# VectorE's order in the q and k blocks, eighteen convolutions of v around their end, and ranks by one comparison per pair

## The chip, the core and the metric

The kernel runs on one core of a Trainium2 chip. The metric is the device time of one execution in microseconds. The engines are TensorE (PE in the profile, its weight loads PEld), VectorE (DVE), ScalarE (ACT), GpSimd (POOL) and SyncE (SP), each with an instruction queue of its own; transfers are issued from the queues of SP, ACT and POOL and run on 16 DMA engines.

## The reference, cut to what matters

The input x is one image of 384 channels and 192 × 192 pixels, float32. Two layers follow one another, each a residual branch on a group norm (32 groups).

```python
# layer 0
qkv = einsum('bchw,oc->bohw', gn(x), w_qkv) + b_qkv          # 1x1 convolution, 384 -> 1152
qkv = qkv.reshape(b, 3*c, 96, 2, 96, 2).max(axis=(3, 5))     # 2x2 max pooling
qkv = depthwise3x3(qkv, w_dw) + b_dw
q, k, v = split(qkv)                                         # 8 heads of 48 channels
q, k = q / max(norm(q), 1e-12), k / max(norm(k), 1e-12)      # norms over the 9216 pixels
attn = einsum('bhcn,bhdn->bhcd', q, k) * temperature         # 48 x 48 per head
out = sum(a_i * topk_softmax(attn, kk) @ v for kk in (24, 32, 36, 38))
x = x + proj(upsample2x(gelu(out)))
# layer 1
x = x + depthwise7x7(gn(x), mean of the four rotations of the weight)
```

`topk_softmax` keeps the kk largest entries of a row; of equal entries the earlier one comes first.

## The kernel before, in words

Channels lie on partitions, 384 of them as three tiles (KT = 3). After the statistics of the first norm (to about 167 us) the norm's scale is folded into `wq`, and q and k are computed in 24 blocks of eight image rows. A block has six channel tiles (three of q, three of k). For each, `pooled` runs three groups of 512 pixels (L663, three matmuls each into a PSUM tile `pq`, of which there are four buffers) and a reduce on VectorE (L673) that takes the maximum of four pixels and writes it into that channel tile's `ring`, a buffer of three blocks of pooled rows with borders. `bordered` has ScalarE copy a row from one end of the ring to the other where it wraps (L695, when the block's number is divisible by three; L699). One block later the nine taps of the depthwise convolution run on VectorE (L706 the first, L708 the eight others). Then comes a 32 × 32 transpose on VectorE (L791), the sum of squares on ScalarE (L719), and, once three tiles of q or of k are there, sixteen copies on ScalarE (`turned`, L725) that complete the transposition into `qkT`. `products` multiplies q by k for pairs of heads into the accumulator `grams` (L741, 24 records per block); they are woven one by one between the matmuls of L663 two blocks later.

`keep` fixes an instruction's place in its engine's order. `pinned` calls it for PE alone: PE's order is written by hand, VectorE's, ScalarE's and GpSimd's orders come from a scheduler that works with modelled times. `issue_after` keeps an instruction from being placed ahead of another.

After the 24th block, the round with b = NB finishes the last taps and starts v. `convolve` is one convolution of v: six matmuls for two strips of two image rows and one channel tile into a `pv` tile (L549, 12 records, two buffers) and one pooling reduce on VectorE into `rows` (L555, called an eviction below). A row group of v is nine such convolutions. The first six stand in the round b = NB, among the last taps; 21 more, up to three row groups (AHEAD = 3), are called together with the steps of `attention`, a generator:

- the norms of q and k and the temperature (L825 to L836), with two small groups of matmuls on PE (L832, L232);
- `scaled` (L841) out of `grams`, ten DMAs that gather the heads' 48 × 48 blocks into `att`, issued in turn from GpSimd and ScalarE, and the scores (L847);
- the rank of each of the 48 entries in its row: for each of three channel tiles five VectorE operations on 48 × 48 = 2304 elements per partition (L866 to L874);
- maximum, exponential (ScalarE), four masked and normalised softmaxes added into `mix` (L879 to L897);
- ten DMAs that lay `mix` out as the block diagonal matrix `diag`, and its transposition on PE into `aT` (L910), evicted as `attnT`.

Between these the scheduler also places the first taps of v (`depthwise_v`, L959 and L963). With `attnT`, a loop over the 16 row groups follows (v, attention, gelu, projection, residual L1076), and then layer 1, in which PE runs the 7 × 7 convolution as matmuls with band matrices (L1482).

Of the kernel before, what the change touches and what calls it, by code (L numbers as in the profile page):

```python
# [8 lines left out]
F32 = mybir.dt.float32  # L9
# [77 lines left out]
def conv_preact_d2(  # L87
# [138 lines left out]
    def along_free(dst, src, pool, name, tag=None):  # L226

        ps = pool.tile([P, C], F32, name=f"af_{name}", tag=tag or f"af_{name}")
        for t in range(KT):
            dg = const.tile([P, P], F32, name=f"dg_{name}_{t}", tag="dg", bufs=KT)  # L230
            nc.vector.tensor_scalar_mul(dg, ident, src[:, t : t + 1])
            nc.tensor.matmul(ps[:, t * P : (t + 1) * P], ones, dg, start=True, stop=True)  # L232
        nc.vector.tensor_copy(dst, ps)
# [329 lines left out]
    with ExitStack() as bx:  # L563
# [78 lines left out]
        def pinned(ins):  # L642

            if ins.ins.engine != mybir.EngineType.PE:
                return ins
            keep(ins)
            while between and next(between[0], between) is between:
# [3 lines left out]
        def pooled(b, ct, xb):  # L651
# [3 lines left out]
            for g in range(3):  # L655
# [17 lines left out]
                nc.vector.tensor_reduce(  # L673
# [4 lines left out]
                )  # L678

# [21 lines left out]
        def taps(dst, ct, win):  # L701
            for tap in range(9):
                src = win(tap // 3, tap % 3)
                w = wd[:, ct, tap : tap + 1]
                if tap == 0:
                    nc.vector.tensor_scalar(dst, src, w, bdb[:, ct : ct + 1], ALU.mult, ALU.add)  # L706
                else:
                    nc.vector.scalar_tensor_tensor(dst, src, w, dst, ALU.mult, ALU.add)  # L708

        def depthwise(b, ct, dst):  # L710
            r0 = b % 3 * PR
            taps(dst, ct, lambda i, j: ring[ct][:, r0 + i : r0 + i + PR, j : j + PS])
# [45 lines left out]
        multiplied = None  # L758
        for b in range(NB + 1):
            xb = None  # L760
            if b < NB:
                xb = held.pop(b) if b in held else load_x(b, "xq")
            else:
# [3 lines left out]
                xb = xpool.tile([P, 2 * UT, KT, RB * HW], F32, name="xv_begun", tag="xb")  # L767
                for kt in range(KT):
                    nc.sync.dma_start(xb[:, :, kt], image_rows(kt, order[0], 0, 2 * UT))
            done, sides = sides, []  # L770
            for ct in range(2 * KT + 1):
                if ct == (KT if b < NB else 1) and done:
                    between.append(products(b - 2, done))
                if b < NB and ct < 2 * KT:
                    if b == 0 and ct < 2:

                        if ct == 0:
                            pooled(b, 0, xb)
                            pooled(b, 1, xb)
                            biases()  # L780
                    else:
                        pooled(b, ct, xb)
                    bordered(b, ct)
                if b > 0 and ct > 0:
                    dst = qkp.tile([P, PR, PS], F32, name=f"qk{b}_{ct}", tag="qk")
                    depthwise(b - 1, ct - 1, dst)
                    s, t = divmod(ct - 1, KT)
                    if t == 0:
                        turns = trp.tile([P, KT, PB], F32, name=f"turns{b}_{s}", tag=f"turns{s}")
                    flat = dst.rearrange("p h w -> p (h w)")  # L790
                    nc.vector.transpose(turns[:, t], flat)  # L791
                    squares(b - 1, ct - 1, flat)

                    for _ in copies:
                        pass
                    if t == KT - 1:
                        side = trp.tile([P, PB // P, C], F32, name=f"qkT{b}_{s}", tag=f"qkT{s}")
                        sides.append(side)
                        copies = turned(side, turns)
                        for _ in range(2):  # L800
                            next(copies)
                    if b == NB:
                        for n in ((), (), (0, 1), (), (2, 3), (4,), (5,))[ct]:
                            t0 = n // KT * UT
# [773 lines left out]
```

## Time and profile before

| what | value |
|---|---|
| median of 3 runs | 2787.28 us (2781.11 to 2789.88) |
| the profiled execution | 2786.69 us, span 2784.9 us |
| mean TensorE clock granted | 0.985 |
| busy PE / DVE / ACT / POOL | 2591.1 / 2456.2 / 1140.1 / 746.7 us |
| q and k: last matmul of L663 ends | 1316.4 us |
| scores (L847) | 1373.16 us |
| attention matrix on PE (L910) starts | 1451.85 us |

A line of a timeline gives the start and the length in us, engine, line and operation, the tile written and the tiles read, shapes, the number of instructions merged into the line, and in brackets how long the engine was idle just before and whose end released it. A group line of the page gives busy us, mean ns of one instruction, and the idle time just before. All times in the text count from the start of the span. A record of L549 or L663 is half a matmul on float32, so that 12 records make a convolution.

### The profile page before, as it was taken

The numbers are of one execution on the slowest core, as the hardware profiler recorded it, in microseconds if no ns is written. First come the engines' busy times: TensorE is split into PE (matmuls) and PEld (weight loads), VectorE is DVE, ScalarE is ACT, GpSimd is POOL, SyncE is SP. The second block draws the span as 40 slices with busy tenths as digits, with TensorE's granted clock in tenths as the row PEclk, the third lists the DMA queues.
The fourth block names the chain that finished last, engine by engine and source line by source line (L and its number), as shares of the span: only waits on it lengthen the run. The fifth ranks groups of instructions, "written<-read, shape, count | busy, mean of one in ns | idle before, by whom it ended". The sixth has DMA issues, their size and how long they took to land. (4 is left out here: it accounts for less than half of the span.)

```text
span 2784.9 us, 25837 instructions
## 1 busy us (share of the span) xinstructions
PE 2591.1 (93%) x8365; PEld 1525.2 (55%) x8365; DVE 2456.2 (88%) x3527; ACT 1140.1 (41%) x2262; POOL 746.7 (27%) x885
## 2 busy tenths in 40 slices
PE   0399999999999999999899969999999899999998
PEld 0144444444444444444556646666666677777776
DVE  7989998989999999999789958999889789888886
ACT  0143423333343333433402312232323577777776
POOL 1024443100000000000111321010101478787876
PEclk9999999999999999999899989999999999999999
DMA  9976766301010110110336997566674899999998
GB/s 381 402 252 217 249 213 228 130 34 68 35 68 35 40 62 35 68 35 0 120 103 238 340 362 231 192 230 219 203 246 151 324 343 366 372 375 372 372 374 264
DMA packets 234039, 581.01 MB, mean 209 GB/s; under 512 B 16640, under 2 KB 165744, under 8 KB 217136
## 3 DMA queue, kind: packets, MB, share of 16 engines
q1 hardware_dynamic: 173408, 283.44, 29.0%
q0 software_dynamic: 37376, 148.85, 15.8%
q10 hardware_dynamic: 23120, 147.07, 14.1%
q8 instruction: 67, 1.10, 0.2%
q14 instruction: 68, 0.56, 0.1%
HBM read 370.93 MB, written 208.21 MB: 208 GB/s over the span
## 5 line engine op out<-in xcount | busy, mean ns | idle before, releaser
L663 PE MATMUL pq<-xq,wq 128*128 128x512 f32 x2268 | 1028.8, 597 | 5.4 <-DVE ring L673 4.7
L708 DVE SCALAR_TENSOR_TENSOR qk<-ring,wd,qk 128x384 f32<-128x384 f32 x1152 | 699.4, 616 | 59.5 <-ACT ring L695 32.1
L663 PEld LDWEIGHTS pq<-xq,wq 128*128 128x128 f32 x2268 | 408.7, 190 | 437.3 <-issue 364.0
L549 PE MATMUL pv<-xv,wq 128*128 128x384 f32 x1656 | 545.7, 490 | 26.0 <-DMA xv<-in_x_dram 21.7
L549 PEld LDWEIGHTS pv<-xv,wq 128*128 128x128 f32 x1656 | 316.7, 192 | 245.8 <-issue 20.4
L1482 PE MATMUL pc<-main,w 128*128 128x288 f32 x1536 | 436.4, 406 | 3.0 <-PE al L1515 1.7
L1502 DVE TENSOR_SCALAR apart<-pc,rb 32x576 f32<-32x576 f32 x384 | 312.1, 813 | 81.2 <-PE pc L1482 55.4
L1482 PEld LDWEIGHTS pc<-main,w 128*128 128x128 f32 x1536 | 290.6, 190 | 87.1 <-issue 2.4
L725 ACT COPY qkT<-turns 32x288 f32<-32x288 f32 x768 | 329.0, 428 | 20.7 <-DVE turns L791 9.3
L1500 ACT ACTIVATE apart<-pc,rb 32x576 f32<-32x576 f32 x384 | 281.1, 732 | 133.5 <-PE pc L1482 128.7
L959 DVE SCALAR_TENSOR_TENSOR vb<-rows,wd,vb 128x576 f32<-128x576 f32 x384 | 313.3, 817 | 11.3
L673 DVE TENSOR_REDUCE ring<-pq 128x128 f32<-128x512 f32 x428 | 292.1, 683 | 3.7 <-PE pq L663 3.6
L1482 PE MATMUL pc<-aux,h 128*128 128x288 f32 x768 | 248.1, 405 | 0.0
L719 ACT ACTIVATE junk<-qk 128x384 f32<-128x384 f32 x144 | 71.1, 494 | 411.8 <-DVE qk L708 411.0
L1441 POOL COPY res<-apart 128x1152 f32<-128x1152 f32 (+1 forms) x96 | 222.0, 2338 | 13.3 <-ACT apart L1500 9.5
L826 POOL TENSOR_TENSOR rn<-rn,halfpos 128x6 f32<-128x6 f32 x1 | 1.4, 1359 | 827.5 <-DVE rn L825 827.5
L1076 DVE TENSOR_TENSOR sx<-xr,y 128x576 f32<-128x576 f32 x180 | 203.8, 1173 | 19.9 <-ACT y L1047 14.8
L555 DVE TENSOR_REDUCE rows<-pv 128x192 f32<-128x768 f32 x144 | 137.7, 957 | 84.7 <-PE pv L549 84.6
L1117 POOL DMA_DIRECT2D sd<-sx x96 | 72.2, 755 | 514.5 <-DVE sx L1076 493.2
L741 PEld LDWEIGHTS grams<-qkT,qkT 128*96 128x96 f32 x576 | 92.8, 165 | 147.3 <-issue 136.1
L1096 ACT ACTIVATE wq<-sx,negmid 128x1152 f32<-128x1152 f32 x96 | 120.6, 1257 | 122.5 <-DVE sx L1076 118.2
L1482 PEld LDWEIGHTS pc<-aux,h 128*128 128x128 f32 x768 | 145.1, 189 | 41.2 <-issue 0.2
(227 smaller groups left out, 2270.6 us busy)
## 6 DMA issues: line engine op xcount, KB each, us to landing
sd<-sx POOLq DMA_DIRECT2D x96, 600.0 KB, 10.1
out_dram<-res SPq DMA_DIRECT2D x192, 288.0 KB, 11.2
main<-sd ACTq DMA_DIRECT2D x46, 1200.0 KB, 6.7
xv<-in_x_dram SPq DMA_DIRECT2D x138, 384.0 KB, 6.6
xr<-in_x_dram SPq DMA_DIRECT2D x45, 1152.0 KB, 11.7
xq<-in_x_dram SPq DMA_DIRECT2D x21, 2304.0 KB, 8.2
w<-wt ACTq DMA_DIRECT2D x46, 1024.0 KB
xs<-in_x_dram SPq DMA_DIRECT2D x24, 1536.0 KB, 15.1
```

The source lines that it names most:

```text
L549: nc.tensor.matmul(ps[:, u, 0 : RB * HW], wq[:, kt, o : o + P], xb[:, u, kt, :], start=(kt == 0), stop=(kt == KT - 1),)
L555: nc.vector.tensor_reduce(rows[ct][:, 1 + t0 : 1 + t0 + UT, 1 : PS + 1], ps[:, :, 0 : RB * HW].rearrange("p u (a w b) -> p u w a b", a=2, ...
L663: ins = nc.tensor.matmul(ps, wq[:, kt, ct * P : (ct + 1) * P], rows[:, kt, :, g * 64 : (g + 1) * 64], start=(kt == 0), stop=(kt == KT - 1) ...
L673: nc.vector.tensor_reduce(t[:, r0 : r0 + PR, 1 + g * 32 : 1 + (g + 1) * 32], ps.rearrange("p (h a w b) -> p h w a b", h=PR, a=2, b=2), AX. ...
L708: nc.vector.scalar_tensor_tensor(dst, src, w, dst, ALU.mult, ALU.add)
L725: nc.scalar.copy(side[f * Q : (f + 1) * Q].rearrange("p c (t n) -> p t c n", n=P)[:, :, :, a * Q : (a + 1) * Q], turns[a * Q : (a + 1) * Q ...
L959: pin(nc.vector.scalar_tensor_tensor(dst, src, w, dst, ALU.mult, ALU.add))
L1076: nc.vector.tensor_tensor(bass.AP(flat.tensor, flat.offset + at(e) + a * RUN, [flat.ap[0], [JP, NT], [1, NJ], [at(f) - at(e), 2]],), xq[:, ...
L1441: keep(copy(res[ps, k], apart[ps, :, k].rearrange("p e n -> p n e")))
L1482: nc.tensor.matmul(ahead[q][:, k, 0 : NT * NJ], lhs, rhs, start=(j == 0), stop=(j == 2), skip_group_check=True,)
L1500: keep(nc.scalar.mul(dst, src, scale))
L1502: keep(nc.vector.tensor_scalar_mul(dst, src, scale))
```

## The change

- **q and k, from the third block on.** `pinned` keeps VectorE's instructions too. The taps are now a generator (`depthwise`), and `pooled` takes two taps after each of its three reduces. The remaining three taps and the transpose of a channel tile (`finish`) come after the next tile's three reduces and six taps. The products join PE's order at the fifth channel tile of a block in place of the fourth. `qkT` of q gets a second buffer.
- **The end of q and k.** Three tiles of `xpool` are filled with x for two whole row groups of v (18 DMAs on SP in place of 3). In the round b = NB each channel tile's nine taps are split four and five, with a convolution after each part (12), `finish` follows one tile late, two convolutions follow the last `finish`, then the norms (moved here out of `attention`), the last products, and four convolutions whose evictions are not kept in place. The products of the block before last join at the third channel tile. Only the third row group's nine convolutions remain beside `attention`.
- **Ranks.** A row of 48 is split in two halves of 24. One comparison of every entry of the second half with every one of the first (576 elements) is summed along both axes; inside the halves one comparison (1152 elements), masked by `lower`, is summed along both axes. Ranks come from these sums and the constant `after`, the number of later entries.

```diff
         def pinned(ins):
-            if ins.ins.engine != mybir.EngineType.PE:
-                return ins
             keep(ins)
-            while between and next(between[0], between) is between:
+            while ins.ins.engine == mybir.EngineType.PE and between and next(between[0], between) is between:
                 between.pop(0)
             return ins
-        def pooled(b, ct, xb):
+        def pooled(b, ct, xb, taps):
             rows = xb.rearrange("p t (r c) -> p t r c", c=HW)
             t = ring[ct]
             r0 = 1 + b % 3 * PR
...
                     )
                     if b > 1:
                         pinned(ins)
-                nc.vector.tensor_reduce(
+                ins = nc.vector.tensor_reduce(
                     t[:, r0 : r0 + PR, 1 + g * 32 : 1 + (g + 1) * 32],
                     ps.rearrange("p (h a w b) -> p h w a b", h=PR, a=2, b=2),
                     AX.XY,
                     ALU.max,
                 )
+                if b > 1:
+                    pinned(ins)
+                some(taps, 2)
...
-        def taps(dst, ct, win):
+        def depthwise(b, ct, dst, pin):
+            r0 = b % 3 * PR
             for tap in range(9):
-                src = win(tap // 3, tap % 3)
+                i, j = divmod(tap, 3)
+                src = ring[ct][:, r0 + i : r0 + i + PR, j : j + PS]
                 w = wd[:, ct, tap : tap + 1]
                 if tap == 0:
-                    nc.vector.tensor_scalar(dst, src, w, bdb[:, ct : ct + 1], ALU.mult, ALU.add)
+                    pin(
+                        nc.vector.tensor_scalar(
+                            dst, src, w, bdb[:, ct : ct + 1], ALU.mult, ALU.add
+                        )
+                    )
                 else:
-                    nc.vector.scalar_tensor_tensor(dst, src, w, dst, ALU.mult, ALU.add)
-        def depthwise(b, ct, dst):
-            r0 = b % 3 * PR
-            taps(dst, ct, lambda i, j: ring[ct][:, r0 + i : r0 + i + PR, j : j + PS])
+                    pin(nc.vector.scalar_tensor_tensor(dst, src, w, dst, ALU.mult, ALU.add))
+                yield
+        def some(taps, n):
+            for _ in range(n):
+                next(taps, None)
...
+        def finish(b, ct, dst, taps, now=False):
+            nonlocal copies, turns
+            some(taps, 9)
+            s, t = divmod(ct, KT)
+            if t == 0:
+                turns = trp.tile([P, KT, PB], F32, name=f"turns{b}_{s}", tag=f"turns{s}")
+            flat = dst.rearrange("p h w -> p (h w)")
+            ins = nc.vector.transpose(turns[:, t], flat)
+            if b > 0:
+                pinned(ins)
+            for _ in copies:
+                pass
+            squares(b, ct, flat)
+            if t == KT - 1:
+                side = trp.tile(
+                    [P, PB // P, C], F32, name=f"qkT{b}_{s}", tag=f"qkT{s}", bufs=2 - s
+                )
+                sides.append(side)
+                copies = turned(side, turns)
+                for _ in range(4 if now else 2):
+                    next(copies)
+        rn = const.tile([P, 2 * KT], F32, name="rn")
+        rkb = const.tile([P, C], F32, name="rkb")
+        def norms():
...
                 pv = psx.enter_context(tc.tile_pool(name="pv", bufs=2, space=PSUM))
...
+                for n in range(3):
+                    t = xpool.tile([P, 2, UT, KT, RB * HW], F32, name=f"xv_begun{n}", tag="xb")
+                    for k in range(2):
+                        i, t0 = divmod((2 * n + k) * UT, NT)
+                        for kt in range(KT):
+                            nc.sync.dma_start(t[:, k, :, kt], image_rows(kt, order[i], t0, UT))
+                        xvb += [(i, t0, ct, t[:, k]) for ct in range(KT)]
+            for ct in range(2 * KT):
+                dst, taps = None, iter(())
+                if b > 0:
+                    dst = qkp.tile([P, PR, PS], F32, name=f"qk{b}_{ct}", tag="qk")
+                    taps = depthwise(b - 1, ct, dst, pinned if b > 1 else lambda ins: ins)
+                if b < NB:
+                    if ct == KT + 1 and b > 1:
+                        done, sides = sides[0:2], sides[2:]
+                        between.append(products(b - 2, done))
                     if b == 0 and ct < 2:
                         if ct == 0:
-                            pooled(b, 0, xb)
-                            pooled(b, 1, xb)
+                            pooled(b, 0, xb, taps)
+                            pooled(b, 1, xb, taps)
                             biases()
                     else:
-                        pooled(b, ct, xb)
+                        pooled(b, ct, xb, taps)
                     bordered(b, ct)
...
+                if last is not None:
+                    finish(*last)
+                    last = None
+                if b > 0:
+                    last = b - 1, ct, dst, taps
+                if b == NB:
+                    if ct == KT - 1:
+                        between.append(products(b - 2, sides[0:2]))
+                    some(taps, 4)
+                    convolve(*xvb.pop(0), pinned)
+                    some(taps, 5)
+                    convolve(*xvb.pop(0), pinned)
+            if b == NB:
+                finish(*last, True)
+                for _ in range(2):
+                    convolve(*xvb.pop(0), pinned)
+                norms()
+                for _ in products(b - 1, sides[2:4]):
+                    pass
+                for args in xvb:
+                    convolve(*args, pe_keep)
...
+        with tc.issue_after(scores.ins):
+            nc.vector.tensor_reduce(after, lower.rearrange("p d e -> p e d"), AX.X, ALU.add)
+        firsts = ap.tile([P, KT, HH], F32, name="firsts")
+        seconds = ap.tile([P, KT, HH], F32, name="seconds")
+        before, behind = [ap.tile([P, KT, HC], F32, name=n) for n in ("before", "behind")]
+        for mt in range(KT):
+            full = [P, HH, HH]
+            sq = ap.tile(full, F32, name=f"sq{mt}", tag="sq")
+            nc.vector.tensor_tensor(
+                sq,
+                att[:, mt, 0:HH].unsqueeze(1).to_broadcast(full),
+                att[:, mt, HH:].unsqueeze(2).to_broadcast(full),
+                ALU.is_ge,
+            )
+            yield
+            nc.vector.tensor_reduce(seconds[:, mt], sq, AX.X, ALU.add)
+            nc.vector.tensor_reduce(
+                firsts[:, mt], sq.rearrange("p d e -> p e d"), AX.X, ALU.add
+            )
+            yield
+            full = [P, 2, HH, HH]
+            halves = att[:, mt, :].rearrange("p (s d) -> p s d", s=2)
+            tri = ap.tile(full, F32, name=f"tri{mt}", tag="tri")
+            nc.vector.tensor_tensor(
+                tri, halves.unsqueeze(2).to_broadcast(full),
+                halves.unsqueeze(3).to_broadcast(full), ALU.is_ge,
+            )
+            yield
+            nc.vector.tensor_tensor(
+                tri, tri, lower.unsqueeze(1).to_broadcast(full), ALU.mult
+            )
+            yield
+            for t, order in ((before, "p s d e -> p s d e"), (behind, "p s d e -> p s e d")):
+                nc.vector.tensor_reduce(
+                    t[:, mt].rearrange("p (s d) -> p s d", s=2), tri.rearrange(order), AX.X,
+                    ALU.add,
+                )
+                yield
+        nc.vector.tensor_tensor(rank, before, behind, ALU.subtract)
+        halves = rank.rearrange("p t (s d) -> p (t s) d", s=2)
+        nc.vector.tensor_tensor(
+            halves, halves, after.unsqueeze(1).to_broadcast([P, 2 * KT, HH]), ALU.add
         )
...
+        nc.vector.tensor_tensor(rank[:, :, HH:], rank[:, :, HH:], seconds, ALU.add)
+        nc.vector.scalar_tensor_tensor(
+            rank[:, :, 0:HH], rank[:, :, 0:HH], float(HH), firsts, ALU.add, ALU.subtract
+        )
+        yield
...
+        for _ in range(9):
+            next(chain, None)
+        i = AHEAD - 1
+        for t0 in range(0, NT, UT):
+            xb = load_v(i, t0)
+            with tc.issue_after(multiplied):
                 for ct in range(KT):
-                    depthwise_v(1, ct, (0, 1))
+                    convolve(i, t0, ct, xb, lambda ins: ins)
+            for _ in range(6):
+                next(chain, None)
+        for ct in range(KT):
+            depthwise_v(1, ct, (0, 1))
```

## The prediction

> **What bounds the kernel now.** I read the page's engine totals first, then the waits of the q/k stretch, then PE's timeline from there to the attention matrix, and last VectorE (DVE) beside it.
>
> ```profile
> PE 2591.1 (93%) x8365; PEld 1525.2 (55%) x8365; DVE 2456.2 (88%) x3527; ACT 1140.1 (41%) x2262; POOL 746.7 (27%) x885
> ...
> PEclk9999999999999999999899989999999999999999
> ```
>
> PE is busy 93% of the span at nearly full clock. The edit can therefore pay only where PE idles or runs slowly. VectorE, at 88%, is close enough to become the bound in a stage. Inside q/k the waits show one defect and the timeline prices it:
>
> ```profile
> DVE qk L708 <- ACT ring L695: 32.1, 32, 2.3
> ```
>
> (what waits, on whom, us in all, times, longest), then PE's timeline and that of all engines:
>
> ```profile
> 749.17 0.33 PE L741 MATMUL grams<-qkT,qkT 128*96 128x96 f32 x2
> ...
> 777.06 22.56 PE L663 MATMUL pq<-xq,wq 128*128 128x512 f32 x50 [0.47 <-DVE ring L673]
> ...
> 799.46 0.33 PE L741 MATMUL grams<-qkT,qkT 128*96 128x96 f32 x2
> ...
> 848.17 0.33 PE L741 MATMUL grams<-qkT,qkT 128*96 128x96 f32 x2
> ```
>
> ```profile
> 767.13 7.02 ACT L725 COPY qkT<-turns 32x288 f32<-32x288 f32 x16
> ...
> 774.17 0.27 ACT L695 COPY ring<-ring 128x96 f32<-128x96 f32 x1
> ...
> 774.48 1.93 DVE L708 SCALAR_TENSOR_TENSOR qk<-ring,wd,qk 128x384 f32<-128x384 f32 x3 [2.05 <-ACT ring L695]
> ```
>
> The first product of a block marks its period: 48.71 us without a stall (799.46 to 848.17), 50.29 with one (749.17 to 799.46). In the longer one, ScalarE's border copy (L695) stands behind sixteen transposed copies of 7.02 us, the last three taps wait 2.05 us for it, the next reduces come late, and PE waits 0.47 us and runs slower for a moment. This falls in every third block. The 21 periods from 256.30 to 1291.52 take 1035.22 us; 21 at 48.71 would be 1022.9, so **12.3 us** are lost.
>
> The second loss follows the last q/k product:
>
> ```profile
> 1303.30 13.07 PE L663 MATMUL pq<-xq,wq 128*128 128x512 f32 x30
> 1322.97 1.65 PE L549 MATMUL pv<-xv_begun,wq 128*128 128x384 f32 x2 [6.61 <-DVE ring L673]
> 1332.45 0.64 PE L741 MATMUL grams<-qkT,qkT 128*96 128x96 f32 x2 [7.84 <-ACT qkT L725]
> ...
> 1344.94 15.67 PE L549 MATMUL pv<-xv_begun,wq 128*128 128x384 f32 x48
> ...
> 1379.45 32.88 PE L549 MATMUL pv<-xv,wq 128*128 128x384 f32 x96 [3.57 <-DVE rows L555]
> 1413.05 38.97 PE L549 MATMUL pv<-xv,wq 128*128 128x384 f32 x120 [0.71 <-DVE rows L555]
> 1451.85 0.93 PE L910 MATMUL aT<-ident,diag 128*128 128x128 f32 x7
> ```
>
> Of the windows, the two rows behind the first gap (busy time of each engine, clock, DMA share, GB/s):
>
> ```profile
> 1323.00:1332.40 9.40, 1.62 (x2) 0.47 (x2) 9.40 (x19) 6.16 (x16) 0.00 (x0) 0.50 0.00 1
> 1332.40:1345.00 12.60, 12.55 (x47) 7.87 (x48) 9.62 (x18) 4.65 (x15) 0.50 (x1) 0.76 0.02 3
> ```
>
> From PE's end of q/k (1316.4, called T0) to the attention matrix (aT, 1451.85) are 135.5 us. The work in it is 110.5: 27 convolutions of v at 3.87 (104.5), products 4.5, norm matmuls 1.5. The other 25 are gaps of 6.61, 7.84, 3.57 and 0.71, and a slow clock (0.50, then 0.76). DVE beside it:
>
> ```profile
> 1373.16 0.31 DVE L847 TENSOR_TENSOR att<-att,rn 128x144 f32<-128x144 f32 x1 [0.24 <-DMA att<-scaled]
> ...
> 1442.46 0.31 DVE L897 TENSOR_TENSOR mix<-mix,em 128x144 f32<-128x144 f32 x1
> ```
>
> and two groups (busy us, mean ns):
>
> ```profile
> L866 DVE TENSOR_TENSOR gt<-att 128x2304 f32<-128x2304 f32 x3 | 7.7, 2553 | 0.0
> ...
> L1076 DVE TENSOR_TENSOR sx<-xr,y 128x576 f32<-128x576 f32 x180 | 203.8, 1173 | 19.9 <-ACT y L1047 14.8
> ```
>
> From the scores (1373.16) to the mixed matrix (1442.77) are 69.6 us of VectorE, 37 of them fifteen rank operations that start 2.47 us apart. The matrix's DMAs land near 1447.8, so in this kernel aT waits for PE's own convolutions.
>
> **The change, part by part.**
>
> *Order in q/k.* Nothing is added or removed. VectorE has 3 reduces (0.60), 8 taps (0.53), one first tap (0.40) and a transpose (0.50) per channel tile: 6.9 us at the pitch of the trace, against 7.73 of PE (three groups of 2.58). The last three taps of a tile now come after the next tile's reduces, about 7.7 us later, so the copy delayed by 7.02 us is there in time. Four PSUM buffers leave PE some 5.5 us before a late reduce stops it, and the products start one tile later, away from the copies that feed them. In a fixed order a late operand stops everything behind it on VectorE, the reduces that PE needs among it; but each operand I followed is there earlier than that. I take all of the stalls as gone: **−12.3**; the other end is 0 (new stalls of the same size).
>
> *Eighteen convolutions beside and behind the end.* In place of 12 convolutions of which PE starts few before VectorE is done, 14 stand before the last products and four behind. SP issues 18 DMAs of two row tiles of x where it issued three of one; each of the three buffers comes free as a q/k block ends, and the last convolution of the third runs at T0 + 77, so I cost them nothing (DMA share in these windows: 0.00 to 0.02; without that cover each late load stops PE for its landing, 6.6 us for a load of this size on the page). Walking PE and DVE by the durations above: PE resumes at T0 + 0.9 and doesn't stop for the products; 14 convolutions (54.2), the interleaved products and small waits end at T0 + 58, norm matmuls and last products at T0 + 61.5. The row-scaled products leave at T0 + 62.3. Their ten DMAs landed in 4.6 to 4.9 us beside x loads; the mix's, alone, in 1.8. The scores are then ready between T0 + 67.3 and T0 + 70; I take 67.3, since the x loads are over by then. This was T0 + 56.8 before: the chain starts **10.5 later**, since more of PE's work stands ahead of it.
>
> *Ranks.* An operation costs about 0.155 + 1.04 ns per element (144 elements 0.305, 2304 elements 2.55), some 0.08 less in pitch: 0.67 for 576, 1.27 for 1152. Per row tile: three of 576 and four of 1152 are 7.1; three tiles 21.3, plus 0.8 for `after` and the sums at the end: 22.1 where there were 37. In the same stretch stand 12 evictions (10.4) where there were 17 (14.8), but 21 taps of v where there were 15 (+4.3); with the small operations the chain is about 53 us where it was 69.6.
>
> *Strided reduces.* Half of the new reduces step 24 numbers per element: 3 × (576 + 1152) + 576 = 5,760 elements. The trace has none. Nearest is L1076, whose reads have gaps: 1.17 us for 576 elements where a dense one takes 0.75, so +0.73 ns per element, +4.2 us. The Trainium skill ("SBUF — State Buffer", "Specifications (TRN2)") speaks against this order: SBUF is read in lines of 16 bytes, each wants two hits, and crossing to another line costs; here every element is on another line. It has no price, so the row gives one. Low end 0; high end three times the row, +12.6. I take **+4.2**.
>
> Sum: 67.3 + 53 + 4.2 = T0 + 124.5 for the mix; the ten DMAs and the start of aT took 5.0: **T0 + 129.5**. The other path, the last eviction (PE ends the 27th convolution at T0 + 111.8) and the 8.4 us of taps and mix behind it, gives T0 + 126, so the chain decides. 135.5 − 129.5: **−6** (−10 without the stride, +2 with its high end).
>
> *The clock.* PE is now idle from T0 + 111.8 to 129.5, 17.7 us, where before it went straight on. The row: after the gap of 7.84 us the clock was 0.50, then 0.76; four cycles of convolution and products took 1.77, 1.76, 1.66 and 1.24 us where warm ones take 0.845, **3.1 us** lost. The skill ("TensorE: Matmul & The Clock Gate", "What's actually happening") has half clock after an idle window of about 3.4 us and until 3.4 us of work have passed: an estimate from it is 1.7 us lost. By the rule the sum is 1.4 better; the trace decides: **+3.1**.
>
> *Behind aT* both programs are alike. The stretch after it (PE waits 22 us there for DMAs near 1640) is fed by transfers that follow aT, so it moves with it: 0.
>
> Sum: −12.3 − 6.0 + 3.1 = **−15.2** on the execution's own 2786.69 (span 2784.9): 2771.5. The median of the runs, 2787.28, is 0.6 above this execution, so I say **2772**.
>
> **The rivals.**
>
> *Full gain (0.22).* The strided reads cost nothing and the DMAs are quick: −12.3 − 10 + 2 = −20, 2767. For: the rank rows show no cost beyond elements. Against: L1076.
>
> *One stall for another (0.17).* VectorE's queue, now rigid, holds at q/k's border copies or squares, so the 12.3 us stay and only the tail's −3 is left: 2784. For: 6.9 of 7.73 us is 90% full. Against: 5.5 us of PSUM slack.
>
> *Slower: the attention chain is laid bare (0.06).* In the old order aT waited for PE, and 4 us of the chain were hidden; now PE is done 18 us before it, so each microsecond of the chain counts in full. The place is the strided reduces; to outweigh the −19.4 of the rest it takes 3.4 ns per element over a dense read, nearly five times the row. At 5 ns: 28.8 − 19.4 = +9, 2796.
>
> *The edit doesn't do what it says (0.04).* If products or convolutions land elsewhere on PE, there is no gain at the tail and perhaps none in q/k: 2787.
>
> **How the numbers follow.** The likeliest case, 2772 (0.51), spans 2768 to 2778 with the scores' DMAs and the stride. Adding full gain and most of the swap of stalls, the range is 2763 to 2784. A measurement of this kernel can tell 0.3%, 8.4 us, from no change. Faster by more: the likeliest and the full gain, and a little of the third, 0.76. Within: most of the third and the fourth, 0.17. Slower: 0.07.
>
> **What would show it.** Right: periods of 48.7 us in all blocks of q/k and no wait for the ring copy; PE without a gap over 1 us from T0 to the 27th convolution; scores near T0 + 67, aT near T0 + 129 after a PE gap of some 18 us; a clock under 0.8 just behind it; strided reduces near 1.8 ns per element. Wrong: periods over 49.5, a new release of PE by the reduces, aT later than T0 + 135, or time lost after aT.

## The result and the profile after

The changed kernel takes 2777.45 us (median of nine runs, 2773.26 to 2779.19), the kernel before 2787.28 in the same session (nine runs, 2778.15 to 2791.79): the medians lie 9.8 us apart, the ratio is 0.9969 (8.6 us), its 95% interval 0.9956 to 0.9982 (5.0 to 12.3 us). The forecast was 2772: the time lies among what its likeliest case allowed (2768 to 2778), but the gain is smaller than the 15.2 us of its sum. The profiled execution took 2777.17 us, span 2775.5, against 2786.69 and 2784.9. So 9.4 us are to be explained on the spans, where 15.2 were forecast.

The page after, and PE's first products of three neighbouring blocks:

```profile
PE 2584.4 (93%) x8365; PEld 1525.9 (55%) x8365; DVE 2449.2 (88%) x3538; ACT 1141.4 (41%) x2262; POOL 744.6 (27%) x885
...
L662 PE MATMUL pq<-xq,wq 128*128 128x512 f32 x2268 | 1021.9, 595 | 0.0
```

```profile
748.88 0.33 PE L751 MATMUL grams<-qkT,qkT 128*96 128x96 f32 x2
...
797.59 0.33 PE L751 MATMUL grams<-qkT,qkT 128*96 128x96 f32 x2
...
846.30 0.33 PE L751 MATMUL grams<-qkT,qkT 128*96 128x96 f32 x2
```

The last column of the group is PE's idle time ahead of q/k's matmuls: none is left. A product marks the period as in the prediction, and all 21 periods, not only these two, are 48.71 us. VectorE's wait for the border copy (32.1 us before) is gone from the list of waits. PE's timeline behind q/k:

```profile
1302.59 8.01 PE L549 MATMUL pv<-xv_begun,wq 128*128 128x384 f32 x24 [0.79 <-DVE ring L672]
1311.83 8.79 PE L549 MATMUL pv<-xv_begun,wq 128*128 128x384 f32 x26 [1.24 <-DVE rows L555]
...
1362.49 2.20 PE L751 MATMUL grams<-qkT,qkT 128*96 128x96 f32 x24
...
1390.08 8.20 PE L549 MATMUL pv<-xv,wq 128*128 128x384 f32 x24 [2.13 <-DVE rows L555]
...
1413.63 8.01 PE L549 MATMUL pv<-xv,wq 128*128 128x384 f32 x24 [0.34 <-DVE rows L555]
1434.82 2.20 PE L990 MATMUL aT<-ident,diag 128*128 128x128 f32 x7 [13.18 <-DMA diag<-mix]
1436.81 13.20 PE L549 MATMUL pv<-xv,wq 128*128 128x384 f32 x36
1449.85 6.21 PE L1095 MATMUL po<-vb,attnT 128*128 128x288 f32 x24
```

The gaps of 6.61 and 7.84 us are gone; at their place PE waits 0.79 and 1.24. In exchange stands a gap of 13.18 ahead of the attention matrix, and the convolutions after it run slowly (13.20 us for 36 records, 11.78 before). The chain on VectorE, and the reduces in it:

```profile
1371.16 0.31 DVE L897 TENSOR_TENSOR att<-att,rn 128x144 f32<-128x144 f32 x1 [1.57 <-DMA att<-scaled]
...
1431.77 0.31 DVE L977 TENSOR_TENSOR mix<-mix,em 128x144 f32<-128x144 f32 x1
```

```profile
L941 DVE TENSOR_REDUCE behind<-tri 128x48 f32<-128x1152 f32 x3 | 9.0, 2998 | 0.0
L923 DVE TENSOR_REDUCE firsts<-sq 128x24 f32<-128x576 f32 x3 | 4.7, 1569 | 0.0
...
L941 DVE TENSOR_REDUCE before<-tri 128x48 f32<-128x1152 f32 x3 | 4.0, 1342 | 0.0
...
L922 DVE TENSOR_REDUCE seconds<-sq 128x24 f32<-128x576 f32 x3 | 2.2, 743 | 0.0
```

`behind` and `before` sum the same 1152 numbers, the one with a stride of 24 numbers (96 bytes), the other densely: 2.998 against 1.342 us. VectorE is busy without a gap from the scores to the mix.

The way from before to after, in milestones: the last q/k matmul ends 14.6 us earlier (1316.37 to 1301.80), the matrix starts 17.0 earlier (1451.85 to 1434.82), the first product with it (`po`) 14.4 earlier (1464.23 to 1449.85), the end of the span 9.4 earlier.

### The profile page after: what moved, and what is told of

Its sections match the earlier page's. It is cut to its first block, busy times and chain, and to the rows that moved or that the text cites. A ratio compares the mean times of both kernels' runs of the same rounds, so it can differ in the third digit from the quotient of the medians.

```text
span 2775.5 us, 25750 instructions
## 1 busy us (share of the span) xinstructions
PE 2584.4 (93%) x8365; PEld 1525.9 (55%) x8365; DVE 2449.2 (88%) x3538; ACT 1141.4 (41%) x2262; POOL 744.6 (27%) x885
## 5 line engine op out<-in xcount | busy, mean ns | idle before, releaser
L549 PE MATMUL pv<-xv,wq 128*128 128x384 f32 x1512 | 500.3, 491 | 29.2 <-DMA xv<-in_x_dram 23.9
L549 PEld LDWEIGHTS pv<-xv,wq 128*128 128x128 f32 x1512 | 289.1, 192 | 231.5 <-issue 22.6
L1405 DVE SCALAR_TENSOR_TENSOR w<-eye,sb,w 128x512 f32<-128x512 f32 x96 | 171.9, 1830 | 1.5
## 6 DMA issues: line engine op xcount, KB each, us to landing
xr<-in_x_dram SPq DMA_DIRECT2D x45, 1152.0 KB, 12.8
```

The costliest lines, as they stand in the source:

```text
L549: nc.tensor.matmul(ps[:, u, 0 : RB * HW], wq[:, kt, o : o + P], xb[:, u, kt, :], start=(kt == 0), stop=(kt == KT - 1),)
L1405: nc.vector.scalar_tensor_tensor(mid, eye.unsqueeze(1).to_broadcast([P, 4, P]), sb[:, c : c + 1], mid, ALU.mult, ALU.add,)
```

## The experiments

All times are medians in us; "matrix" is the start of L910/L990, in brackets how long behind the last q/k matmul; "x waits" is what PE waits for x between 1480 and 1720 us. These columns come from one profile each, and profiles of the same code differ by some us at the end of q/k. A batch is a set of kernels that ran together. The three batches ran on different chips, so a kernel is compared with the others of its batch, or by its ratio. The ratio is an estimate over all executions and can differ from the quotient of the medians by up to 0.1%. Batch 1 has no execution of the changed kernel; there it is compared by its ratio from the first session, which is weaker.

| kernel | median | ratio to before, 95% | last q/k | matrix | first `po` | x waits |
|---|---|---|---|---|---|---|
| before, first session | 2787.28 | 1 | 1316.4 | 1451.9 (135.5) | 1464.2 | 21.7 |
| after, first session | 2777.45 | 0.9969 (0.9956 to 0.9982) | 1301.8 | 1434.8 (133.0) | 1449.9 | 23.9 |
| batch 1: before | 2786.06 | 1 | | | | |
| qk_only | 2781.37 | 0.9982 (0.9972 to 0.9992) | 1300.8 | 1444.5 (143.7) | 1456.9 | 23.0 |
| old_ranks | 2778.48 | 0.9972 (0.9962 to 0.9981) | 1301.4 | 1441.4 (140.1) | 1456.1 | 17.5 |
| late_taps | 2765.31 | 0.9923 (0.9908 to 0.9938) | 1301.9 | 1421.6 (119.7) | 1441.2 | 17.2 |
| delay12 | 2789.97 | 1.0017 (1.0009 to 1.0025) | 1304.1 | 1453.5 (149.4) | 1468.4 | 22.1 |
| batch 2: before | 2762.49 | 1 | | | | |
| after_again | 2749.18 | 0.9957 (0.9942 to 0.9972) | 1304.4 | 1437.4 (133.0) | 1452.0 | 2.1 |
| dense | 2738.69 | 0.9920 (0.9898 to 0.9942) | 1304.0 | 1428.8 (124.7) | 1443.9 | 0.0 |
| qk_kept | 2755.99 | 0.9982 (0.9972 to 0.9992) | 1302.4 | 1444.5 (142.1) | 1456.9 | 0.8 |
| best | 2742.03 | 0.9934 (0.9909 to 0.9960) | 1300.7 | 1420.5 (119.8) | 1439.3 | 1.2 |
| batch 3: before | 2761.50 | 1 | | | | |
| after_third | 2746.01 | 0.9939 (0.9927 to 0.9952) | 1304.1 | 1437.1 (133.0) | 1451.6 | 0.0 |
| new_ranks_only | 2764.65 | 1.0006 (0.9992 to 1.0020) | 1311.8 | 1450.0 (138.2) | 1462.3 | 1.3 |
| tree | 2746.52 | 0.9935 (0.9917 to 0.9954) | 1300.0 | 1424.8 (124.8) | 1439.2 | 0.4 |
| tree_late1 | 2742.79 | 0.9926 (0.9913 to 0.9938) | 1301.2 | 1421.6 (120.4) | 1437.5 | 1.9 |

**The order in q/k alone.** `finish` and the taps keep the changed order up to the 24th block; the round b = NB, `attention` and the ranks are those of before.

```diff
             else:
...
+                finish(*last)
+                between.append(products(b - 2, sides[0:2]))
+                for ct in range(2 * KT):
+                    dst = qkp.tile([P, PR, PS], F32, name=f"qk{b}_{ct}", tag="qk")
+                    finish(b - 1, ct, dst, depthwise(b - 1, ct, dst, pe_keep), pe_pinned)
+                    for n in ((), (0, 1), (), (2, 3), (4,), (5,))[ct]:
+                        t0 = n // KT * UT
+                        convolve(0, t0, n % KT, xb[:, t0 : t0 + UT], pe_pinned)
```

> The changed kernel's order of VectorE in the q and k blocks, with the end of q and k, the attention function and the ranks of the kernel before. Theory A (the gain lies in the q/k order, and the changed tail brings 2 to 3 us at most): every block 48.71 us, the last q/k matmul some 14 us earlier than before, the tail from there to the attention matrix about 135 us as before; the whole 9 to 14 us faster than before. Rival B (the tail carries the gain; without it the q/k gain is given back in the gaps behind the last block): under 4 us faster than before.

The last q/k matmul moved as expected, but the tail grew from 135.5 to 143.7 us, and only 5.0 us arrived (0.9982). That is near Rival B. Was it an accident of PE's order, in which the norm's small matmuls had gone ahead of the products? In qk_kept they are kept behind them (the three of L232 in the same way):

```diff
-            nc.tensor.matmul(
+            keep(nc.tensor.matmul(
                 tps[:, t : t + 1], hsel[:, t * P : (t + 1) * P], tmpr, start=True, stop=True
-            )
+            ))
```

> As qk_only, with the six small matmuls of the norms kept behind the last products on PE. Theory A (qk_only lost 8 us in its tail because these matmuls went ahead of the products and held them up): the matrix starts 4 to 8 us earlier than in qk_only, the whole is 8 to 12 us faster than before. Rival D (VectorE reaches the end of q/k as late as before whatever PE does, so that an earlier end of PE is waited away): within 1 us of qk_only at the matrix.

It was not: the matrix starts at the same time (1444.50 against 1444.53), and the ratio is the same 0.9982. By its number Rival D holds, and VectorE's timeline shows why. The last reduce and the last transpose of q/k in the kernel before, then in qk_kept:

```profile
1322.22 0.70 DVE L673 TENSOR_REDUCE ring<-pq 128x128 f32<-128x512 f32 x1
...
1343.40 0.58 DVE L791 STREAM_TRANSPOSE turns<-qk 128x384 f32<-128x384 f32 x1
```

```profile
1302.82 0.68 DVE L672 TENSOR_REDUCE ring<-pq 128x128 f32<-128x512 f32 x1
...
1343.75 0.58 DVE L784 STREAM_TRANSPOSE turns<-qk 128x384 f32<-128x384 f32 x1
```

In these profiles PE is done 14 us earlier, VectorE at the same moment. The new order serves PE's reduces first and puts taps off; in the kernel before, the last reduce came at 1322.22 and 21 us of VectorE's work followed it, in qk_kept 41 us. PE then waits for it:

```profile
1317.81 0.63 PE L751 MATMUL grams<-qkT,qkT 128*96 128x96 f32 x2 [13.33 <-ACT qkT L735]
...
1349.74 0.64 PE L751 MATMUL grams<-qkT,qkT 128*96 128x96 f32 x2 [4.99 <-ACT qkT L735]
```

In the changed kernel the last transpose is at 1354.35, 10.6 us later than in qk_kept, which is about the price of the twelve evictions put ahead of it (12 × 0.87), and the scaled products leave VectorE at 1364.79, where before they left at 1364.95. So most of the PE time that the order alone gains is owed by VectorE and waited away: of 14 us 7.3 are left at the matrix and 5.0 in time. The convolutions put into it, with the old ranks (old_ranks, below, in the batch of qk_only), bring the matrix 3.1 us further forward (1441.4 against 1444.5); in time 0.9972 against 0.9982 does not tell the two apart.

**The ranks alone.**

```diff
-        lower = ap.tile([P, HC, HC], F32, name="lower")
...
-            nc.vector.tensor_tensor(gt, other, mine, ALU.is_gt)
...
+        rank = ap.tile([P, KT, HC], F32, name="rank")
+        after = ap.tile([P, HH], F32, name="after")
...
```

> The kernel before with the new ranks alone, 6 us less work for VectorE between scores and mix. Theory A (in the old order the matrix waits for PE's own convolutions, and the chain has 4 us to spare): the matrix starts within 2 us of before, the whole within 3 us. Rival F (VectorE decides there too): the matrix 4 to 6 us earlier, the whole 4 to 6 us faster.

```profile
1411.05 39.07 PE L549 MATMUL pv<-xv,wq 128*128 128x384 f32 x120 [0.34 <-DVE rows L555]
1449.96 0.93 PE L946 MATMUL aT<-ident,diag 128*128 128x128 f32 x7
```

1.0006 (0.9992 to 1.0020): nothing, as theory A has it. PE's convolutions run up to the matrix without a gap, as they did before. Then the other way round, the changed kernel with the ranks of before (the two blocks above exchanged):

> The changed kernel with the ranks computed as before (five operations on 2304 elements per tile, 37 us). The new rank operations take 31.0 us by the durations of the changed kernel's trace, strided reduces included. Theory A (VectorE's chain decides when the attention matrix starts, since PE has nothing left): the matrix starts some 6 us later than in the changed kernel, and the whole is 4 to 6 us slower than it. Rival B (the ranks are hidden beside the convolutions, as they were before): within 1 us of the changed kernel.

```profile
1441.43 2.20 PE L954 MATMUL aT<-ident,diag 128*128 128x128 f32 x7 [15.93 <-DMA diag<-mix]
```

The matrix starts 6.6 us later than in the changed kernel, and PE waits for it, as theory A has it, so the chain decides there. The 4 to 6 us that theory A wanted in time are not seen: 0.9972 against 0.9969, with intervals of ±0.1%, which leaves it open; the profile has 6.4 us less waiting for x further on.

**More work in the chain.**

```diff
+            if mt == KT - 1:
+                for _ in range(12):
+                    nc.vector.tensor_tensor(
+                        tri, tri, lower.unsqueeze(1).to_broadcast(full), ALU.mult
+                    )
             yield
```

> The changed kernel with twelve more multiplications of the third tile's comparison by the mask, which is idempotent (1.27 us each, 15.2 us of VectorE ahead of the mix's end; the result is unchanged). Theory A (time behind the matrix moves with it): 13 to 15 us slower than the changed kernel. Rival C (the transfers behind the matrix give part back whatever starts them): 9 us slower or less, with less idle PE in the stretch near 1640 us.

```profile
1453.54 2.19 PE L995 MATMUL aT<-ident,diag 128*128 128x128 f32 x7 [31.01 <-DMA diag<-mix]
```

The twelve took 16.2 us, and the matrix starts 16.4 us later behind the last q/k matmul (149.4 against 133.0); PE's gap ahead of it grew from 13.18 to 31.01. By the ratios the kernel is 4.7 us above before (1.0017), where the changed kernel is 8.6 below (0.9969): 13.3 us, some four more or less by the two intervals. That is theory A. What is added to VectorE here is paid in full at the matrix, and for the greater part in time.

**The stride.**

```diff
-                firsts[:, mt], sq.rearrange("p d e -> p e d"), AX.X, ALU.add
+                firsts[:, mt], sq, AX.X, ALU.add
...
-            for t, order in ((before, "p s d e -> p s d e"), (behind, "p s d e -> p s e d")):
+            for t, order in ((before, "p s d e -> p s d e"), (behind, "p s d e -> p s d e")):
```

and the same for `after`.

> The changed kernel with its seven strided reduces summing along the dense axis (the ranks are then sums over the wrong axis; instructions, shapes and waits are the same). Theory A (the gap between the numbers costs 1.44 ns each, 8.3 us of VectorE's chain, and the chain decides): these reduces take 0.74 and 1.34 us as the others do, the matrix starts 8 us earlier, the whole is 4 to 8 us faster than the changed kernel. Rival B (the chain is hidden): the matrix starts within 1 us of the changed kernel's. Rival E (the slow part is the reduce into 24 or 48 sums, not the gap): they stay at 1.57 and 3.0 us.

Groups of dense, and its matrix:

```profile
L941 DVE TENSOR_REDUCE behind<-tri 128x48 f32<-128x1152 f32 x3 | 4.0, 1342 | 0.0
L922 DVE TENSOR_REDUCE seconds<-sq 128x24 f32<-128x576 f32 x3 | 2.2, 745 | 0.0
L923 DVE TENSOR_REDUCE firsts<-sq 128x24 f32<-128x576 f32 x3 | 2.2, 743 | 0.0
```

```profile
1428.77 2.20 PE L990 MATMUL aT<-ident,diag 128*128 128x128 f32 x7 [11.50 <-DMA diag<-mix]
```

The same reduces now take 1.342 and 0.743 us, so it was the stride; the matrix starts 8.3 us less behind the last q/k matmul (124.7 against 133.0), and the kernel is 10.5 us faster than after_again on the same chip. Theory A, a little above its range; Rivals B and E fall.

**The order of VectorE's work behind the scores.**

```diff
-        for ct in range(KT):
-            depthwise_v(1, ct, (0, 1))
         for _ in chain:
             pass
+        with tc.issue_after(mixed[-1]):
+            for ct in range(KT):
+                depthwise_v(1, ct, (0, 1))
```

> The changed kernel with the first taps of v (27 VectorE operations, 21 of them ahead of the mix's end) placed behind the last operation of the mix. Theory A (VectorE, not the order of its work, is the bound from the scores to the first product with the attention matrix): the matrix starts some 13 us earlier with no idle PE ahead of it, but the first product with it waits for the taps, and only the 4 to 8 us in which VectorE idled behind the mix are won: 3 to 7 us faster than the changed kernel. Rival B (the order is at fault): 11 to 14 us faster. Rival C (the transfers behind the matrix set the end): nothing.

```profile
1421.56 0.49 PE L992 MATMUL aT<-ident,diag 128*128 128x128 f32 x3
...
1425.22 7.91 PE L549 MATMUL pv<-xv,wq 128*128 128x384 f32 x24
1435.49 5.83 PE L549 MATMUL pv<-xv,wq 128*128 128x384 f32 x12 [2.37 <-DVE rows L555]
1441.16 6.21 PE L1098 MATMUL po<-vb,attnT 128*128 128x288 f32 x24
```

The matrix starts 13.3 us earlier with no gap ahead of it and no slow clock behind (24 records in 7.91 us). The first product with it is only 8.7 us earlier, since VectorE, busy throughout, is behind with evictions: theory A's mechanism. The time moved more, from 0.9969 to 0.9923, 12.8 us by the ratios, which is B's number. In the two profiles the difference of 15.4 us is these 8.7 and 6.7 us of shorter x waits; these vary from profile to profile (17 to 24 us in the first session and batch 1), so B's number is no sign of B's mechanism. The taps are not paid later: from the first to the fourth `po` late_taps takes 148.4 us, as after_third does. best takes two more costs off VectorE:

```diff
+            if i % 2 == 0:
+                sent = gather.ins
+        with tc.issue_after(sent):
+            lower = ap.tile([P, HH, HH], F32, name="lower")
...
+        for e in range(HC // 2):
+            nc.gpsimd.memset(after[:, e : e + 1], float(HC // 2 - 1 - e))
```

> As late_taps, and two costs taken off VectorE's chain: the gathers of the scores stand ahead of two memsets and a select on GpSimd (1.8 us), and the constant `after` is written by memsets early on (1.5 us of a strided reduce). Theory A (VectorE is the bound from the scores to the first product with the matrix): the scores are 1.8 us earlier, the mix 3.3 us, the first product 2 to 3 us, and the whole is 1 to 4 us faster than late_taps. Rival C (transfers behind the matrix set the end): no change from late_taps.

```profile
1420.50 0.93 PE L996 MATMUL aT<-ident,diag 128*128 128x128 f32 x7
```

Counted from the last q/k matmul, the mix is done 2.8 us earlier than in late_taps (113.7 against 116.5), but the matrix starts no earlier (119.8 against 119.7): it stands behind PE's 27th convolution without a gap, so here PE's own work is the bound again. The first product comes at 138.6 (139.3 in late_taps), less of a gain than expected. In time, 0.9934 (0.9909 to 0.9960) against 0.9923 on another chip tells nothing between the two; within its batch its median is 7.2 us below after_again's, with intervals that overlap.

**Both together.** tree has the ranks without a strided reduce:

```diff
+        for t in (tris, sqs):
+            for n in (12, 6, 3, 1):
+                nc.vector.tensor_tensor(
+                    t[:, :, 0:n], t[:, :, 0:n], t[:, :, n : 2 * n], ALU.add
+                )
+                yield
```

with the gathers and `after` of best; tree_late1 also puts `depthwise_v(1, KT - 1, (0, 1))` behind the mix.

> The changed kernel itself beside the others of this batch, as their reference on this chip: 9 to 13 us faster than before.

> The changed kernel with the same ranks and no strided reduce: the sums over the outer axis are made by halving, with additions of dense rows over all three tiles at once (1.87 us for 1728 numbers, then 0.97, 0.52, 0.22 and so on: 5.9 us where six strided reduces took 13.2); `after` is written by memsets early on, and the gathers of the scores stand ahead of the memsets on GpSimd. Theory A (VectorE's chain decides): scores 1.8 us and mix 10 us earlier than in the changed kernel, the matrix near 123 us behind the last q/k matmul, the whole 8 to 10 us faster than the changed kernel. Rival G (many small dependent operations and longer ones delay the evictions, so that PE's convolutions become late): 3 to 5 us.

> As tree, with the nine operations of one of the three channel tiles' first taps (6.6 us) placed behind the mix, where VectorE idles some 8 us waiting for the matrix. Theory A: the matrix starts right behind the 27th convolution, some 120 us behind the last q/k matmul, with no idle PE and no slow clock, and the first product with it some 135 us behind: 2 to 5 us faster than tree. Rival (VectorE gives it back behind the matrix, as with all taps late): within 1.5 us of tree.

after_third is 15.5 us faster than before, above its expectation. tree's matrix starts 124.8 us behind the last q/k matmul, close to theory A, and its first `po` is 8.3 us less behind it than in after_third; tree_late1's matrix 120.4, its `po` 136.3. But tree's median is that of after_third, against an expectation of 8 to 10 us, and tree_late1's is 3.2 us lower, with intervals that overlap. In the profiles the gain is there when layer 1's convolution begins (the L1482 of the kernel before: 2158.93 in tree, 2170.21 in after_third), and more than half of it is spent in it: from there to the end of the span tree takes 583.1 us, after_third 576.5. Of these 6.6 us, 3.7 pass up to the convolution's last matmul and 2.9 behind it. A wait that after_third does not have at all, in tree:

```profile
POOL res L1534 <- DMA out_dram<-res: 41.2, 18, 7.0
```

GpSimd waits there for the output's transfers. best and late_taps have this wait too (62.5 and 50.6 us) but take 576.9 and 577.6, so it isn't shown to be the cause; tree's six runs also spread over 15 us (2736.67 to 2752.13). A rival that no run tests is that the transfers set the pace of layer 1: from 2200 to 2700 us the DMA engines are full in all of these kernels (share 1.01 to 1.02, at 365 GB/s in tree and 369 in after_third). This stays open.

**The changed kernel again.**

> The changed kernel itself, once more, beside the others of this batch. If the stretch near 1640 us gives back a part of an earlier start by a rule, PE's waits for x there sum to 24 us again; if they differ from execution to execution, another sum between 17 and 24 us is seen with the same start, and only medians over many runs can be compared. Median within 3 us of 2777.

The median of 2749 is far from the 2777 expected, but so is the kernel before on this chip (2762). The start of the matrix behind the last q/k matmul is the same to 0.1 us in all three profiles of the changed kernel (133.0), but the x waits are not: 23.9, 2.1 and 0.0. In the first session and in batch 1 every profile has 17 to 24 us of them, in batches 2 and 3 every one 0 to 2. It goes with the batch, and so perhaps with the chip (that of the first session is not known), not with the kernel. The windows of the stretch (second to last figure the DMA share, last GB/s), before in the first session and then after_third:

```profile
1500.00:1650.00 150.00, 138.92 (x476) 90.03 (x474) 130.56 (x149) 40.23 (x90) 47.77 (x64) 0.97 1.00 351
```

```profile
1500.00:1650.00 150.00, 149.95 (x510) 96.31 (x509) 135.81 (x155) 41.33 (x90) 47.16 (x63) 1.00 1.00 367
```

With the DMA engines full in both, one moves 351 GB/s and PE waits; the other moves 367 and it doesn't. These are two kernels, but the changed kernel alone shows the same: in this window its engines, full too, moved 343 GB/s in the first session, 365 in after_again and 367 in after_third. Why, is not shown. The kernel before takes 2786 to 2787 us where PE waits for x, and 2762 where it doesn't.

## Why the prediction was right, and where its sum was off

*The q/k stalls.* Right: all periods are 48.71 us. The last q/k matmul is 14.6 earlier: the 12.3 of the sum, 0.5 because q/k's first matmul came earlier, and 1.8 from the blocks ahead of the first period counted. These last 2.3 are not the change's doing. new_ranks_only has the q/k code of the kernel before; its 21 periods lose 10.2 us, and its last q/k matmul ends at 1311.8, 4.6 before that of the first profile. The twelve profiles with the new order end it between 1300.0 and 1304.4. So the end of q/k moved by 7 to 16 us from profile to profile, of which the stalls are 10 to 12. What the prediction had not seen is that this term is not worth its 12.3 by itself: qk_only and qk_kept gain 5 us each, since VectorE ends q/k no earlier than before.

*The tail.* Forecast 129.5 us from the last q/k matmul to the matrix; measured 133.0, so the term was −2.5 in place of −6. PE's part was close up to the products (resumed at 0.8, products over at 62.9 in place of 61.5); behind them PE waits up to 2.13 us for evictions, against the forecast of no gap over 1 us, and the 27th convolution ends at 119.8 in place of 111.8. The chain without the strided excess was right: 52.6 us in place of 53. (The terms written down for it add up to 54.6; the old chain also held three waits of 0.45 us for PE, which are gone.) The mis-sized terms are three. The strided reduces: +4.2 in the sum, taken from L1076's 0.73 ns per element; the rows give 0.83 us more for 576 elements and 1.66 for 1152, 8.3 us in all (1.44 ns), which dense confirms. That is 4.1 us more than the sum had, its largest error. The Trainium skill's rule on lines of 16 bytes ("SBUF — State Buffer", "Specifications (TRN2)") spoke the right way, with no price; L1076 was a poor stand-in for a stride of 24. The scores: 69.4 us behind, in place of 67.3. The gathers did land in 1.6 to 1.8 us, but those of GpSimd were issued late, behind two memsets and a select that the scheduler had placed ahead of them:

```profile
1364.82 0.58 POOL L885 MEMSET lower<- 128x576 f32 x1 [8.27 <-PE grams L751]
1365.34 1.05 POOL L980 MEMSET diag<- 128x1152 f32 x1
1366.35 0.84 POOL L886 TENSOR_SCALAR_AFFINE_SELECT lower<-lower 128x576 f32<-128x576 f32 x1
1367.15 2.61 POOL L896 DMA_DIRECT2D att<-scaled  x5
```

In best and tree, where these gathers go first, the scores come at 68.2, so 1.2 of the 2.1 us are shown to be this order's.

And, the other way, the matrix starts 2.7 us behind the mix, not 5.0: its first transposes go as soon as their blocks have landed, though its seven then take 2.20 us where they took 0.93.

*The clock.* Forecast a gap of 17.7 us and 3.1 lost; the gap is 13.2, since evictions on VectorE held the last convolutions back, and the convolutions behind the matrix lost 1.4 (13.20 − 11.78); in the window from 1434.80 to 1440.00 the clock is 0.53: it is 0.50 up to 1438.50 and 1.00 from 1440.00. The matrix's own 1.3 more us are partly the wait for its DMAs, partly this clock. In the seven profiles with a gap of 11.5 to 31.0 us ahead of the matrix the convolutions behind it lost 0.8 to 1.5. The estimate of 1.7 from the Trainium skill's rule ("TensorE: Matmul & The Clock Gate", "What's actually happening": half clock until some 3.4 us of work have passed) was nearer than the row of before, where convolutions and products had been interleaved; there a second gap of 7.84 us followed 1.65 us of work.

*Behind the matrix.* Forecast 0. In the first session's profiles, 14.4 us at the first `po` are 9.4 at the end: 2.2 in longer waits for x, the rest in smaller amounts up to the end of layer 1. In the batches without those waits the changed kernel is 13.3 and 15.5 us faster by the medians (0.9957 and 0.9939), about what the sum said. The interval of after_again overlaps with that of the first session (5.0 to 12.3 us); that of after_third (13.3 to 20.2) does not. So the gain does differ between sessions, but that the waits for x take back a part is not shown: no run changes them alone.

*The sum as a whole.* At the first `po` 15.2 us were forecast and 14.4 measured. That this is so close is partly luck: 2.3 us came from what stands ahead of the first period, and the shorter start of the matrix and the milder clock made up for about half of what the strided reduces and the scores cost beyond the sum.

*The rivals.* "Full gain" fell with the price of the strided reduces. "One stall for another" was wrong for PE in q/k, and, for VectorE at the end of q/k, near the truth: the taps put off had to be done there. "The chain is laid bare" named the right place: the chain does decide when the matrix starts, and what is put on it or taken off it showed in time in delay12 and dense, though not in old_ranks and tree. The price of the strided reduces was 8.3 us, not the 19.4 at which the change would have lost.

## What to carry to other kernels

A fixed order that serves the bound engine first does not remove work from the engine that feeds it: look at when that other engine ends the stage, and see what the first can do meanwhile. When filler work is moved ahead of a chain, the chain behind it is bare: what is put on it or taken off it, other engines' memsets ahead of its DMAs too, moves its end, until the bound engine's own work ends later (best). A dense sum over an outer axis by halving is cheaper than a reduce with a stride (the ranks took 7.3 us less in tree), but take such a gain as won only when it shows in the time of several runs: some 8 us at the first product arrived in dense and not in tree. And before a difference between two profiles is put down to a change, look how far two profiles of the same code lie apart: at the end of q/k it was 4.6 us.

## What the runs showed of the hardware

A reduce on VectorE over 1152 float32 numbers with a stride of 96 bytes takes 2.998 us, a dense one 1.342; over 576, 1.569 and 0.743. The stride more than doubles it. And the rate at which full DMA engines served the same kernel in the same window differed between sessions by 7% (343 GB/s where PE waits for x, 365 and 367 where it waits little or not at all); the cause is not shown.
